# A graph layer on one core: raw input rows gathered in the head, columns copied in two groups of five, single tiles fetched row by row on SyncE

## The chip, the cores and the metric

The kernel runs on one core of one Trainium2 chip. The metric is device time in microseconds of one execution, taken as the median of several runs. A separate execution was profiled; its trace supplies all rows below.

## The reference

12,500 nodes carry 64 features; 412,500 edges, sorted by receiver, carry 32. All is float32.

```python
h = relu(layernorm(x))
msg_in   = concat(h[src], h[dst], edge)            # 64 + 64 + 32
messages = silu(msg_in @ W1 + b1) @ W2 + b2
logits   = silu(msg_in @ Wa1 + ba1) @ Wa2 + ba2
att      = softmax(logits, axis=0)                 # over all edges
agg      = segment_sum(messages * att, dst)
out      = x + silu(concat(h, agg) @ Wu1 + bu1) @ Wu2 + bu2
```

## The kernel before

**Head.** L170 to L313 read x in 8 chunks, normalise it, and transpose it into `hT` (node features in columns, two nodes' features above each other in the 128 partitions). `senders` (L259) multiplies `hT` with the sender half of both first layers and writes one 128-wide row per node to `ts_d` in HBM; the loop at L300 does the same for receivers into `tr_d`, adding the bias, and issues its DMAs from ScalarE's queue. L313 also writes `hT` itself to `hT_d` (used only in a fallback pass).

**Main loop.** The edges lie in tiles of 128, eight tiles to a group, 403 groups. For a group `g`:

- `load(g)` (L524) runs two groups ahead (`AHEAD = 2`). GpSimd issues one indirect DMA for each tile (L533): 128 rows of `ts_d`, chosen by `src`, into the tile `gs`. There are 7 such buffers. SyncE loads the edge features and receiver numbers once per four groups (L544, L547) and two windows of `tr_d` per group (L554) at an address from a register. VectorE builds a one-hot matrix of receivers (L558), and TensorE multiplies it with the window (L562) into `pe` in PSUM.
- `begin(g)` (L570): VectorE adds `pe` and `gs` (L573), ScalarE takes the tanh (L576).
- `end(g)` (L578): VectorE forms the messages and the logits (L586 to L597) in four passes of 512 columns. silu is made of tanh, a sum and a product, on weights that are halved.
- `sum_up` (L714) handles the group five steps older: eight weighted one-hots on VectorE (L640), eight matmuls (L646), a copy of the sum out of PSUM on ScalarE (`out_of`, L652), a projection (L657), and an addition into the running sums in SBUF (`put`, L660).

**Chosen groups.** In every third group (127 of them) the eighth tile isn't gathered. SyncE loads its 128 sender numbers (`numbers`, L474), VectorE turns them into column numbers of `hT` (`places`, L481, six operations), and ScalarE reads these into registers and copies 128 columns of `hT`, one instruction each (`columns`, L504), in six bursts over three steps. One matmul with `stack` (L568) then makes the eighth tile's rows, after VectorE has masked the wrong half (L567). `begin` needs an extra copy for that tile (L575).

**Tail.** After the last group the node update runs over 13 tiles of up to 8 x 128 nodes (L825 to L866): exp of the running maxima (`factor`, ScalarE), a product (`first`, VectorE, two instructions), a sum on GpSimd, tanh and a product (`silu`), matmuls of 128 rows with block-diagonal weights (`second`), and a sum with x (`rest`), then the output DMAs.

**What orders the work.** Each engine and each queue takes its instructions in program order, and nearly all are pinned to the order of the text. A buffer's reuse, a tile's landing and each of the rotating DMA semaphores are waited for at the issuing instruction. So a DMA on SyncE that waits for a buffer holds back everything that SyncE issues behind it.

Of the kernel before, what the change touches and what calls it, by code (L numbers as in the profile page):

```python
# [44 lines left out]
F32 = mybir.dt.float32  # L45
I32 = mybir.dt.int32
# [7 lines left out]
P = 128  # L54
# [14 lines left out]
B = 4  # L69
NQ = 4  # L70
# [3 lines left out]
EVERY = 3  # L74
PHASE = 1
SLOTS = (((0, 24), (24, 24)), ((48, 24), (72, 12)), ((84, 24), (108, 20)))
# [7 lines left out]
PARTS = [("pair", 4 * C), ("we", C), ("bias", C), ("wu2h", 2 * D), ("wa2", U), ("bu2", D), ("w_bu", U),  # L84
         ("w2b", U), ("wu1a", U), ("wu2", D), ("ba2", 1), ("w_bup", 2 * U), ("bu1", 1)]
HALVED = 4
# [4 lines left out]
def gnn_kernel(ctx: ExitStack, tc: tile.TileContext, n_edges, x, src, src_row, dst, dst_row, first, edge,  # L91
# [14 lines left out]
    hT_d = dram.tile([2 * D, NB // 2, P], F32, name="hT_d")  # L106
# [19 lines left out]
    w_bu = part["w_bu"][:D + 1]  # L126
# [25 lines left out]
    nc.vector.memset(zero, 0.0)  # L152

# [8 lines left out]
    gather = ctx.enter_context(tc.tile_pool(name="gather", bufs=7))  # L162


    with tc.tile_pool(name="node1", bufs=1) as node1, \
            tc.tile_pool(name="node", bufs=2) as node, \
            tc.tile_pool(name="node_ps", bufs=2, space=PSUM) as node_ps:
        x_v = x.rearrange("(p b) d -> p b d", b=NB)

# [10 lines left out]
        nc.sync.dma_start(src_full, src)  # L180
# [11 lines left out]
        def windows():  # L192
# [6 lines left out]
            pin(nc.vector.tensor_tensor(dloc[:, T - K:], dloc[:, T - K:], real, ALU.mult))  # L199
            for h in range(2):  # L200
                pin(nc.vector.tensor_scalar(bj[:, :, h], base_full, iota_p, float(SHIFT * h),
                                            op0=ALU.add, op1=ALU.add))
# [13 lines left out]
        def subtract(i):  # L216

            n = chunks[i][1]
            total = node.tile([P, CB], F32, name="total")[:, :n]
            pin(nc.vector.tensor_reduce(total, xcs[i], AX.X, ALU.add))  # L220
            xm = xms[i] = node.tile([P, CB, D], F32, name="xm", bufs=3)[:, :n, :]
            pin(nc.vector.scalar_tensor_tensor(xm, total[:, :, None].to_broadcast([P, n, D]), -1.0 / D,
                                               xcs[i], op0=ALU.mult, op1=ALU.add))
# [34 lines left out]

        def senders(i, first, last):  # L259
# [6 lines left out]
            for b in range(first, last, 4):  # L266
                m = min(4, last - b)
                pn = node_ps.tile([P, 4, C], F32, name="pn", bufs=4)
                for k in range(0, m, 2):
                    pin(nc.tensor.matmul(pn[:, k:k + 2, :], hT[:, (c + b + k) // 2, :],  # L270
                                         w_pair[:, 0], start=True, stop=True))
                pin(nc.scalar.copy(ts[:, b:b + m, :], pn[:, :m, :]))
            if last == nn:
                pin(nc.sync.dma_start(
                    ts_d.rearrange("(p b) f -> p b f", b=NB)[:, c:c + nn, :], tss.pop(i)))

# [5 lines left out]
        for i in range(nch + 1):  # L282
            if i < nch:
                totals(i)
# [12 lines left out]
            if i < nch:  # L297
                normal(i)
        windows()
        for c, nn in chunks:  # L300
            tr = node.tile([P, CB, C], F32, name="tr")[:, :nn, :]
            for b in range(0, nn, 4):
                n = min(4, nn - b)
                pn = node_ps.tile([P, 4, C], F32, name="pn", bufs=4)
                for i in range(0, n, 2):
                    pin(nc.tensor.matmul(pn[:, i:i + 2, :], hT[:, (c + b + i) // 2, :],
                                         w_pair[:, 1], start=True, stop=True))
                pin(nc.vector.tensor_tensor(tr[:, b:b + n, :], pn[:, :n, :],
                                            bias[:, None, :].to_broadcast([P, n, C]), ALU.add))
            pin(nc.scalar.dma_start(  # L310
                tr_d[:NP, :].rearrange("(p b) f -> p b f", b=NB)[:, c:c + nn, :], tr))
        pin(nc.scalar.dma_start(tr_d[NP:, :], zero[:WR, :]))
        pin(nc.scalar.dma_start(hT_d, hT))  # L313
# [6 lines left out]


def node_bias(tc, b, v, work, ps):

    nc = tc.nc
    NB, w_bu = v["NB"], v["w_bu"]
    n = min(4, NB - b)
    hb = work.tile([D + 1, 4, P], F32, name="hb")
    nc.vector.memset(hb[D:, :, :], 1.0)
    for r in range(2):
        nc.sync.dma_start(hb[:D, r:n:2, :], v["hT_d"][r * D:(r + 1) * D, b // 2:(b + n) // 2, :])  # L330
    pb = ps.tile([P, 4, P], F32, name="mt")
    nc.tensor.matmul(pb[:U, :n, :], w_bu, hb[:, :n, :], start=True, stop=True)
    return pb[:U, :n, :]


def tile_bias(tc, c, first, v, work, ps, bus):
# [12 lines left out]
    to = bus[c].rearrange("u (h k p b) -> u k h p b", h=2, k=2, b=m // 2)  # L349
    for b in range(i, i + n):  # L350
        r, k = b % 2, b // (m // 2)
        if b >= i + 2 and m // 2 > 1:
# [3 lines left out]
        at = b - k * (m // 2)  # L356
        pin(nc.vector.tensor_scalar(  # L357
            to[:, k, :, :, at:at + 2 * q - 1:2],
# [12 lines left out]
def halves(ap, c, n, k, NB):  # L371

    return ap.rearrange("(h p b) d -> p h b d", h=2, b=NB)[:, :, c + k * n // 2:c + (k + 1) * n // 2, :]


def tile_rest(tc, c, step, v, work, rest):
# [3 lines left out]
    if step == 0:  # L380
        xt = rest[c] = work.tile([P, 4 * P], F32, name="xt", bufs=1)[:, :n * D]
        for k in range(2):
            nc.sync.dma_start(
                xt[k * P // 2:(k + 1) * P // 2].rearrange("p (h b d) -> p h b d", h=2, d=D),
                halves(v["x"], c, n, k, v["NB"]))
# [8 lines left out]
def one_pass(tc, n_edges, v):  # L394
# [9 lines left out]
    ACTS, WINS, AHEAD = 8, 3, 2  # L404

    starts = list(range(0, NG - 11, B)) + [NG - 11, NG - 9] + list(range(NG - 7, NG))
    NS = len(starts)
# [4 lines left out]
    with ExitStack() as ctx:  # L412
# [6 lines left out]
        bases = keep.tile([33, NG + 1], I32, name="bases")  # L419
        base_lo, base_hi = bases[0:1], bases[32:33]  # L420
        nc.vector.memset(base_lo, 0)
        nc.vector.memset(base_hi, 0)
        nc.vector.tensor_scalar(base_lo[:, :NG], base_sb[:, :NG], float(NH), float(W),
                                op0=ALU.min, op1=ALU.add)
        nc.vector.tensor_scalar(base_hi[:, :NG], base_sb[:, :NG], float(W - NH), 0.0,
                                op0=ALU.add, op1=ALU.max)
        nmax = keep.tile([P, NS + 1], F32, name="nmax")
        nc.vector.memset(nmax[:, 0:1], BIG)
        scale = keep.tile([P, NS], F32, name="scale")
        total = keep.tile([P, 1], F32, name="total")  # L430
        nc.vector.memset(total, 0.0)
        start = keep.tile([P, 2], F32, name="start")
        nc.vector.memset(start[:, 0:1], 0.0)
        nc.vector.memset(start[:, 1:2], BIG)
        ones = keep.tile([P, P], F32, name="ones")
        nc.vector.memset(ones, 1.0)
# [4 lines left out]
        stack = keep.tile([2 * D, C], F32, name="stack")  # L441
        nc.vector.tensor_tensor(stack, v["w_pair"][:, 0, :C], v["w_pair"][:, 0, C:], ALU.add)
        half = keep.tile([P, 1], F32, name="half")
        nc.vector.memset(half[:D], 0.0)
        nc.vector.memset(half[D:], 1.0)
        w2u = keep.tile([S1, 2, U], F32, name="w2u")
        acts = [keep.tile([EP, K, S1], F32, name=f"acts{i}") for i in range(ACTS)]
        for a in acts:
            nc.vector.memset(a[:, :, U:S1], 1.0)
        wins = [keep.tile([P, 2, 2, C], F32, name=f"wins{i}") for i in range(WINS)]  # L450
        for w in wins:
            nc.vector.memset(w, 0.0)
            for r in range(2):
                rows = slice(WR + r * DE, WR + (r + 1) * DE)
                nc.vector.tensor_copy(w[rows, :, r, :], we[rows, None, :].to_broadcast([DE, 2, C]))
        with tc.tile_pool(name="work2", bufs=2) as work2, \
# [3 lines left out]
            pes, gss, lgs, ps_, psums, sps, pps, ees, mts, nums, cols = ({} for _ in range(11))  # L460


            w2t_ps = one_ps.tile([P, 4, P], F32, name="mt")[:U, 0, :S1]
            nc.tensor.transpose(w2t_ps, w2b, ident[:S1, :S1])
            w2t = small.tile([U, S1], F32, name="w2t", bufs=1)
            nc.vector.tensor_copy(w2t, w2t_ps)
            w2u_ps = one_ps.tile([P, 4, P], F32, name="mt")[:S1, 0, :U]
            nc.tensor.matmul(w2u_ps, w2t, wu1a, start=True, stop=True)
            for h in range(2):
                nc.vector.tensor_copy(w2u[:, h, :], w2u_ps)  # L470

            chosen = {g for g in range(8, NG - 12) if g % EVERY == PHASE}

            def numbers(g):  # L474
                if g in chosen:
                    e = (g * K + K - 1) * EP
                    n = nums[g] = small.tile([P, EP], I32, name="num", bufs=2)
                    nc.sync.dma_start(n, bass.AP(tensor=v["src_row"].tensor,
                                                 offset=v["src_row"][:, e:].offset, ap=[[0, P], [1, EP]]))

            def places(g):  # L481
                if g not in chosen:
                    return
                n = nums[g]
                near = small.tile([1, EP], F32, name="near", bufs=1)
                to = small.tile([1, EP], I32, name="to", bufs=2)
# [654 lines left out]
```

## Time and profile before

| | us |
|---|---|
| median of 3 runs | 3992.78 (3986.42 to 3993.82) |
| the profiled execution's own time | 3986.92 |
| its span in the trace | 3985.1 |
| PE / weight loads busy | 2332.9 / 1888.3 |
| VectorE (DVE) busy | 3264.8 |
| ScalarE (ACT) busy | 2173.0 |
| GpSimd (POOL) busy | 2950.2 |

Busy leaves out instructions that only read registers, branch, wait or issue a DMA from SP or ACT; the indirect DMAs on POOL are counted as busy. "Idle before" in a group's row is the time in which its engine did nothing before an instruction of that group, with what ended it; "issue" means that it waited for nothing that the trace shows. SPq is SyncE's queue, PEld the weight loads. L numbers are lines of the kernel before.

### The profile page before, as it was taken

How to read it: one execution, taken by the hardware profiler on the slowest of the kernel's cores; microseconds unless marked ns; L12 is line 12 of the kernel's file. 1: busy time of each engine (PE TensorE's matmuls, PEld its weight loads, DVE VectorE, ACT ScalarE, POOL GpSimd, SP SyncE). 2: the span in 40 equal slices, each digit the busy share in tenths (PEclk: the TensorE clock that was granted, in tenths of full speed). 3: DMA queues.
4: the chain of work that ended last, by engine and by line, in shares of the span. 5: the costliest groups of instructions: out<-in, count | busy, mean ns of one | idle time of the engine just before them, and what ended most of it. 6: DMA issues, size and time to landing. Idle time of an engine off the chain costs nothing. (4 is left out here: it accounts for less than half of the span.)

```text
span 3985.1 us, 80416 instructions
## 1 busy us (share of the span) xinstructions
PE 2332.9 (59%) x11238; PEld 1888.3 (47%) x11238; DVE 3264.8 (82%) x9553; ACT 2173.0 (55%) x17477; POOL 2950.2 (74%) x3122
## 2 busy tenths in 40 slices
PE   6556566666666555555555555555655555555566
PEld 5444444454444444444444444444544444444455
DVE  6888888888888787888878888887878887878787
ACT  3655555555555555555555555555555555555512
POOL 3777777777777777777777777777777777777774
PEclk8766666666666666666666666666666665666666
DMA  8333343333333333333333333333333333333333
GB/s 287 101 99 99 95 110 92 103 99 102 102 92 95 93 85 93 87 92 88 89 94 84 95 93 86 94 84 94 88 91 94 84 95 87 91 95 84 104 105 85
DMA packets 219778, 391.64 MB, mean 98 GB/s; under 512 B 72209, under 2 KB 146898, under 8 KB 206050
## 3 DMA queue, kind: packets, MB, share of 16 engines
q0 software_dynamic: 99104, 203.16, 19.1%
q1 hardware_dynamic: 118754, 173.60, 16.7%
q10 hardware_dynamic: 1376, 9.67, 0.6%
q14 instruction: 452, 3.70, 0.3%
q8 instruction: 92, 1.51, 0.2%
HBM read 360.42 MB, written 25.72 MB: 97 GB/s over the span
## 5 line engine op out<-in xcount | busy, mean ns | idle before, releaser
L533 POOL DMA_INDIRECT gs<-ts_d,src_sb x3097 | 2933.0, 947 | 992.6 <-issue 854.1
L562 PE MATMUL pe<-wins,eo 128*128 128x256 f32 x3224 | 1465.1, 630 | 925.7 <-DVE eo L558 679.6
L504 ACT COPY cols<-hT 128x1 f32 x16256 | 1605.0, 187 | 717.7 <-issue 714.8
L562 PEld LDWEIGHTS pe<-wins,eo 128*128 128x128 f32 x3224 | 970.9, 318 | 1222.7 <-DVE eo L558 769.0
L576 ACT ACTIVATE pe<-gs 128x1024 f32<-128x1024 f32 x403 | 413.7, 1026 | 928.6 <-DVE gs L573 496.8
L573 DVE TENSOR_TENSOR gs<-pe,gs 128x1024 f32<-128x1024 f32 (+1 forms) x403 | 475.4, 1180 | 393.6 <-DMA gs<-ts_d,src_sb 369.2
L640 DVE TENSOR_SCALAR wt<-iota_w,dloc,p 128x40 f32<-128x40 f32 x3224 | 726.1, 321 | 1.8
L646 PE MATMUL sp<-wt,acts 128*65 128x40 f32 x6448 | 628.8, 268 | 6.3 <-DVE wt L640 3.9
L646 PEld LDWEIGHTS sp<-wt,acts 128*65 128x65 f32 x6448 | 589.9, 183 | 16.2 <-DVE wt L640 9.7
L657 PEld LDWEIGHTS mt<-ss,w2u 65*128 65x128 f32 x806 | 203.0, 279 | 336.2 <-issue 173.9
L657 PE MATMUL mt<-ss,w2u 65*128 65x40 f32 x806 | 181.6, 319 | 242.3 <-DVE gm L623 202.0
L616 PE MATMUL mt<-ident,mx 128*128 128x128 f32 x107 | 47.4, 443 | 445.8 <-DVE sums L675 427.2
L594 DVE TENSOR_TENSOR pe<-pe,w_all 128x512 f32<-128x512 f32 x403 | 281.8, 699 | 13.4
L558 DVE TENSOR_SCALAR eo<-dbs,bj 64x256 f32<-64x256 int32 x806 | 277.9, 375 | 18.2 <-DMA dbs<-in_dst_row_dram 9.0
L592 DVE SCALAR_TENSOR_TENSOR pe<-pe,gs 128x512 f32<-128x512 f32 x403 | 280.3, 696 | 10.5
L586 DVE SCALAR_TENSOR_TENSOR acts<-pe,gs 128x512 f32<-128x512 f32 x403 | 277.2, 688 | 12.4 <-ACT pe L576 3.2
L597 DVE TENSOR_REDUCE lg<-pe 128x8 f32<-128x512 f32 x403 | 277.0, 687 | 10.5
L616 PEld LDWEIGHTS mt<-ident,mx 128*128 128x128 f32 x107 | 19.5, 182 | 456.9 <-issue 455.0
L678 DVE COPY stand<-nmax 64x40 f32 x806 | 161.0, 200 | 3.2
L671 DVE SCALAR_TENSOR_TENSOR sums<-sums,scale,mt 64x40 f32 x214 | 54.2, 253 | 89.2 <-PE mt L657 85.0
L675 DVE TENSOR_TENSOR sums<-sums,mt 64x40 f32 x592 | 111.5, 188 | 4.7 <-PE mt L657 0.6
L357 DVE TENSOR_SCALAR bu<-mt,w_all 64x256 f32<-64x256 f32 (+1 forms) x50 | 23.9, 477 | 88.7 <-PE mt L348 88.3
(124 smaller groups left out, 1062.7 us busy)
## 6 DMA issues: line engine op xcount, KB each, us to landing
eo<-in_edge_dram SPq DMA_DIRECT2D x100, 512.0 KB
dbs<-in_dst_row_dram SPq DMA_DIRECT2D x200, 256.0 KB
gs<-ts_d,src_sb POOLq DMA_INDIRECT x3097
wins<-tr_d SPq DMA_DIRECT2D x806, 32.0 KB
num<-in_src_row_dram SPq DMA_DIRECT2D x127, 64.0 KB
ts_d<-ts SPq DMA_DIRECT2D x5, 896.0 KB
tr_d<-tr ACTq DMA_DIRECT2D x5, 896.0 KB
hT_d<-hT ACTq DMA_DIRECT2D x1, 3136.0 KB
```

The costliest lines, as they stand in the source:

```text
L504: pin(nc.scalar.copy(to[:, first + i:first + i + 1], hT[:, bass.ds(regs[i], 1)]))
L533: nc.gpsimd.indirect_dma_start(out=full[:rows, j, :], out_offset=None, in_=ts_d[:, :], in_offset=bass.IndirectOffsetOnAxis(ap=src_full[:ro ...
L558: pin(nc.vector.tensor_scalar(eo[:WR, e], db[:, e], bj[g // NQ % 2 * WR:(g // NQ % 2 + 1) * WR, g, h:h + 1], None, op0=ALU.is_equal))
L562: pin(nc.tensor.matmul(pe[:, 2 * q:2 * q + 2, :], eo[:, q * EP:(q + 1) * EP], win[:, q // 2, :, :], start=True, stop=q < H - 1 or g not in ...
L573: pin(nc.vector.tensor_tensor(gss[g][:, :n, :], pes[g][:, :n, :], gss[g][:, :n, :], ALU.add))
L576: pin(nc.scalar.activation(pes[g], gss[g], AF.Tanh))
L586: pin(nc.vector.scalar_tensor_tensor(acts[g % ACTS][:, :, 0:U], th[:, :, U:C], 1.0, gs[:, :, U:C], op0=ALU.add, op1=ALU.mult))
L592: pin(nc.vector.scalar_tensor_tensor(att, th[:, :, 0:U], 1.0, gs[:, :, 0:U], op0=ALU.add, op1=ALU.mult))
L594: pin(nc.vector.tensor_tensor(att, att, wa2[:EP, None, :].to_broadcast([EP, K, U]), ALU.mult))
L640: pin(nc.vector.tensor_scalar(wt[:, j, :], iota_w[:EP, j // H, :], dloc[:, g * K + j:g * K + j + 1], p[:, k + j:k + j + 1], op0=ALU.is_equ ...
L646: pin(nc.tensor.matmul(sp, acts[g % ACTS][:, j, :], wt[:, j, :], start=j == 0, stop=j == K - 1))
L657: pin(nc.tensor.matmul(pp, w2u.rearrange("s h u -> s (h u)"), sps.pop(g), start=True, stop=True))
```

## The change

Five things are changed at once.

1. **Raw rows in the head.** The first four groups (`RAW = 4`) no longer use `ts_d`. In the head GpSimd gathers 32 tiles of 64-wide rows of x itself, into two of the gather buffers; ScalarE and VectorE normalise them, TensorE transposes them, and in `load(g)` for `g < 4` four more matmuls with `w_pair` make the senders' part. `gather` has 6 buffers in place of 7, `acts` 6 in place of 8; `begin` writes to a tile `sm` of its own, so that a gather buffer is free after `begin`, not after `end`.
2. **Columns in two of five groups**: 153 groups in place of 127 (`g % 5` 0 or 3, from 10 on), in ten equal half steps. The column numbers are made once, before the loop, for all groups (`column_lists`: two rounds of load, six VectorE operations, two stores to `list_d`); per chosen group SyncE then fetches one row of numbers (`listed`) and one broadcast row of parities (`parity`).
3. **Rows on SyncE**: in one group of eleven (33 by the formula in the code, 22 to 374) the eighth tile is fetched by 128 DMAs of one 512-byte row each, addressed by registers, 12 per step, spread over the eleven steps before.
4. **The head and out_of**: constants are set up early; the sender and receiver matmuls are split into halves of 64 rows; `tr_d` is written from SyncE; `hT_d` is gone; the copy out of PSUM in `out_of` moves from ScalarE to VectorE.
5. **Tail**: all 13 exps first and in place, one product per tile, ScalarE's `Silu` in place of tanh and a product, matmuls of 64 rows, one output layout for both halves.

```diff
-EVERY = 3
-PHASE = 1
-SLOTS = (((0, 24), (24, 24)), ((48, 24), (72, 12)), ((84, 24), (108, 20)))
+EVERY = 5
+LEADS = {0: 9, 3: 10}
+SLOTS = ((0, 28), (28, 24), (52, 28), (80, 24), (104, 24))
+FIRST = 10
+ROWS = 12
+SPAN = -(-EP // ROWS)
+RAW = 4
...
+        for g in range(RAW):
+            for j in range(K):
+                nc.gpsimd.indirect_dma_start(
+                    out=raws[g // 2][:, g % 2, j, :], out_offset=None, in_=x[:, :],
+                    in_offset=bass.IndirectOffsetOnAxis(ap=src_full[:, g * K + j:g * K + j + 1], axis=0))
...
+        def rows_of(pn, r, c, m):
+            for k in range(m // 2):
+                for h in range(2):
+                    rows = slice(h * D, (h + 1) * D)
+                    pin(nc.tensor.matmul(pn[:, h, k, :], hT[rows, c // 2 + k, :],
+                                         w_pair[rows, r, h * C:(h + 1) * C], start=True, stop=True))
...
+        def raw_squares(a):
+            flat = raws[a].rearrange("p r k d -> p (r k) d")
+            spare = node_ps.tile([P, 4, P], F32, name="pt")[:, 0, :D]
+            for i in range(RD):
+                pin(nc.scalar.activation(spare, flat[:, i, :], AF.Square, bias=raw_sum[a][:, i:i + 1],
+                                         accum_out=raw_sq[a][:, i:i + 1]))
...
-        pin(nc.scalar.dma_start(hT_d, hT))
...
+            def rows(g):
+                r, i = (g + 2) // SPAN + 1, (g + 2) % SPAN
+                of = [c for c in rowed if c // SPAN == r]
...
+                at, n = i * ROWS, min(ROWS, EP - i * ROWS)
...
+                loads, regs = nc.values_load_multi_w_load_instructions(
+                    places[of[0]][0:1, at:at + n], engines=[ENG.SP], min_val=0, max_val=NP - 1,
...
+                for k in range(n):
+                    pin(nc.sync.dma_start(single[of[0]][at + k:at + k + 1, :], ts_d[bass.ds(regs[k], 1), :]))
...
-                for j in range(K - (g in chosen)):
+                for j in range(0 if g < RAW else K - (g in chosen or g in rowed)):
...
+                    if g < RAW:
+                        turned = v["raws"][g // 2][:, g % 2].rearrange("p k d -> p (k d)")
+                        pin(nc.tensor.matmul(pe[:, 2 * q:2 * q + 2, :], turned[:, q * EP:(q + 1) * EP],
+                                             v["w_pair"][:, 0], start=False, stop=True))
...
+                sm = sms[g] = work2.tile([EP, K, C], F32, name="sm", bufs=2)
...
-                pin(nc.scalar.copy(ss, sp))
+                pin(nc.vector.tensor_copy(ss, sp))
...
-                numbers(g + 7)
-                places(g + 6)
+                listed(g + 9)
+                rows(g)
+                asked(g + SPAN + 5)
+                parity(g + 5)
...
-                pin(nc.scalar.activation(th, ut, AF.Tanh, scale=0.5))
-                pin(nc.vector.scalar_tensor_tensor(ut, th, 1.0, ut, op0=ALU.add, op1=ALU.mult))
+                pin(nc.scalar.activation(ut, ut, AF.Silu))
...
-                    pin(nc.tensor.matmul(po[:, i, :, :], uv[:, i], wu2h, start=True, stop=True))
+                    for h in range(2):
+                        rows = slice(h * U, (h + 1) * U)
+                        pin(nc.tensor.matmul(po[:, h, i * D:(i + 1) * D], uv[rows, i],
+                                             wu2h[rows, h, :], start=True, stop=True))
```

More of the change, by code (lines that the diff above doesn't have):

```diff
@@ L265, in senders @@
             ts = tss[i]
[L266 to L272, printed above, removed]
+            for b in range(first, last, 8):
+                m = min(8, last - b)
+                pn = node_ps.tile([P, 2, 4, C], F32, name="pn", bufs=3)
+                rows_of(pn, 0, c + b, m)
+                pin(nc.scalar.copy(ts[:, b:b + m, :].rearrange("p (k h) c -> p h k c", h=2), pn[:, :, :m // 2, :]))
             if last == nn:
@@ L403, in one_pass @@
         v[k] for k in ("wa2", "ba2_c", "w2b", "wu1a", "wu2h", "we", "gather"))
[L404 to L407 removed]
+    AHEAD = 2
+    starts, NS, nmax, total, start, ones, half, bases, acts, wins, stack, w2u = (
+        v[k] for k in ("starts", "NS", "nmax", "total", "start", "ones", "half", "bases", "acts", "wins",
+                       "stack", "w2u"))
     batch = [sum(1 for i in starts if i <= g) - 1 for g in range(NG)]
@@ L459, in one_pass @@
                 tc.tile_pool(name="one_ps", bufs=1, space=PSUM) as one_ps:
[L460 to L468, printed above, removed]
@@ L496, in columns @@
-            def columns(g, first, n):
-                if g not in chosen:
-                    return
-                to, at = cols[g]
-                _, regs = nc.values_load_multi_w_load_instructions(
-                    at[0:1, first:first + n], engines=[ENG.Activation], min_val=0, max_val=NP // 2 - 1,
+            pes, gss, lgs, ps_, psums, sps, pps, ees, mts, lists, odds, cols, sms, single, places = ({} for _ in range(15))
+            chosen = [g for g in range(FIRST, NG - 12) if g % EVERY in LEADS]
@@ new lines, in columns @@
+            def columns(g, first, n):
+                if first == 0:
+                    cols[g] = small.tile([P, EP], F32, name="cols", bufs=2)
+                loads, regs = nc.values_load_multi_w_load_instructions(
+                    lists[g][0:1, first:first + n], engines=[ENG.Activation], min_val=0, max_val=NP // 2 - 1,
+                    skip_runtime_bounds_check_because=WHY)
+                for one in loads:
+                    pin(one)
+                for i in range(n):
+                    pin(nc.scalar.copy(cols[g][:, first + i:first + i + 1], hT[:, bass.ds(regs[i], 1)]))
```

334 lines of the change are left out of this document (194 added, 140 removed).

## The prediction

> **What bounds the kernel now.** First the page: the span and the busy times, then the costliest group, then the waits of POOL and DVE, then the timeline around the first and the last gather.
>
> ```profile
> span 3985.1 us, 80416 instructions
> PE 2332.9 (59%) x11238; PEld 1888.3 (47%) x11238; DVE 3264.8 (82%) x9553; ACT 2173.0 (55%) x17477; POOL 2950.2 (74%) x3122
> L533 POOL DMA_INDIRECT gs<-ts_d,src_sb x3097 | 2933.0, 947 | 992.6 <-issue 854.1
> ```
> ```profile
> POOL gs L533 <- issue: 854.1, 2802, 0.3
> ...
> DVE gs L573 <- DMA gs<-ts_d,src_sb: 369.2, 175, 6.5
> ...
> POOL gs L533 <- DMA ts_d<-ts: 47.4, 1, 47.4
> POOL gs L533 <- DMA gs<-ts_d,src_sb: 46.9, 149, 1.8
> ```
> ```profile
> 49.82 1.10 POOL L533 DMA_INDIRECT gs<-ts_d,src_sb  x1 [47.43 <-DMA ts_d<-ts]
> ...
> 3927.03 0.94 POOL L533 DMA_INDIRECT gs<-ts_d,src_sb  x1 [0.30 <-issue]
> ```
>
> DVE has the highest share, yet it waits 369.2 us for gathers, while POOL hardly waits for anybody: its idle time is 0.3 us of issue behind nearly each gather, one wait for `ts_d`, and 46.9 us in all for earlier gathers to land. From first to last gather pass 3877.2 us, 1.2523 us for each of 3096 steps. So the stream of gathers on POOL is the time: 49.8 us ahead of it, 3877.2 in it, and 58.1 from the last gather to the end. A group costs 3097/403 x 1.2523 = 9.62 us.
>
> **The change, part by part.**
>
> *Fewer gathers.* 3224 tiles less 32 (raw), 153 (columns) and 33 (rows) leave 3006 in the stream, 91 fewer than before. The groups from 10 on have 2958; at 1.2523 a step of these groups costs 9.43 us on average, 8.77 where a tile is left out. Whether POOL stays the bound depends on the other engines' steps.
>
> *DVE.* It loses `places`, gains `out_of`, and 26 more masks and copies.
>
> ```profile
> L567 DVE SCALAR_TENSOR_TENSOR cols<-num,half,cols 128x128 f32<-128x128 int32 x127 | 43.6, 343 | 2.0
> L490 DVE TENSOR_SCALAR near<-near 1x128 f32<-1x128 f32 x127 | 37.4, 294 | 4.3
> L492 DVE SCALAR_TENSOR_TENSOR to<-to,near 1x128 int32<-1x128 int32 x127 | 36.3, 286 | 4.3
> L575 DVE COPY gs<-pe 128x128 f32<-128x128 f32 x127 | 35.5, 280 | 0.0
> L491 DVE TENSOR_SCALAR near<-near 1x128 f32<-1x128 f32 x127 | 32.7, 257 | 4.3
> ...
> L487 DVE TENSOR_SCALAR to<-num 1x128 int32<-1x128 int32 x127 | 32.4, 255 | 2.0
> L489 DVE TENSOR_SCALAR near<-to 1x128 f32<-1x128 int32 x127 | 31.4, 247 | 4.3
> ...
> L493 DVE TENSOR_SCALAR num<-num 128x128 int32<-128x128 int32 x127 | 27.4, 216 | 0.0
> ...
> L466 DVE COPY w2t<-mt 64x65 f32<-64x65 f32 x1 | 0.2, 208 | 0.0
> ```
> ```profile
> L573 DVE TENSOR_TENSOR gs<-pe,gs 128x1024 f32<-128x1024 f32 x276 | 337.2, 1222 | 345.2 <-DMA gs<-ts_d,src_sb 325.5 <-issue 14.2 <-PE pe L562 4.4
> ...
> L573 DVE TENSOR_TENSOR gs<-pe,gs 128x896 f32<-128x896 f32 x127 | 138.2, 1088 | 48.4 <-DMA gs<-ts_d,src_sb 43.6
> ```
>
> `places` is L487 and L489 to L493: 197.6 us go. `out_of` adds 403 x 0.208 = 84. The new groups add 26 x (0.343 + 0.280 - 0.134) + 33 x (0.280 - 0.134) = 18. DVE ends near 3170 busy, 7.9 us a step. Nothing of this is on the path, since 9.43 covers it.
>
> *ACT.* It loses `out_of` and gains 26 x 128 column copies.
>
> ```profile
> L504 ACT COPY cols<-hT 128x1 f32 x16256 | 1605.0, 187 | 717.7 <-issue 714.8 <-DVE pe L592 2.9
> ...
> L576 ACT ACTIVATE pe<-gs 128x1024 f32<-128x1024 f32 x403 | 413.7, 1026 | 928.6 <-DVE gs L573 496.8 <-DVE gs L575 238.9 <-DMA gs<-ts_d,src_sb 187.9
> ```
>
> A chosen group costs (1605.0 + 717.7)/127 = 18.29 us with its register reads; 153 cost 2798. With tanh 413.7 and about 75 us of small exps that is 3287, or 8.2 us a step. The 928.6 us that ACT waited ahead of tanh shrink by about half, and 1.2 us a step remain. Queued behind a late burst is the next tanh, and DVE's messages wait for that; between `begin` and the messages DVE has the one-hots of two later steps to make (L558, L640), which hide a tanh that is late by a little.
>
> *SP.* Each of 363 steps (9 to 371) gets 11.6 row DMAs and a read of 12 registers.
>
> ```profile
> L554 SPq FUSED_REGOPS  x806: 37/37/51, 78.2 to 3889.7; - x162
> L554 SPq MOVE wins<-tr_d x806: 29/29/123, 78.3 to 3889.8; - x162
> L554 SPq DMA_DIRECT2D wins<-tr_d x806: 316/317/1517, 78.4 to 3889.8; - x162
> ```
> ```profile
> L547 SPq DMA_DIRECT2D dbs<-in_dst_row_dram x202: 332/412/1539, 74.0 to 3836.9; - x101
> ```
> ```profile
> 2003.74 0.85 SPq L554 DMA_DIRECT2D wins<-tr_d  x2
> 2003.78 1.21 ACT L504 COPY cols<-hT 128x1 f32 x12 [0.73 <-issue]
> ```
>
> A DMA at a register's address takes 37 + 29 + 317 ns, 0.38 us, at least; two of them took 0.85 us from the first's start to the second's end, so one follows another after 0.53. The trace has no one-row DMA; the two-window DMA is the nearest row, and I take 0.52. Twelve registers cost ACT 0.73 us. SP's step: windows 1.04, rows 6.05, registers 0.78, `listed` and `parity` 0.36, a quarter of the three loads and four registers 0.45: **8.7 us**, with 7.1 and 10.0 as ends: 0.38 a row without any gap, and 0.63 where a row is as slow to issue as `dbs` (412 ns for 317). I stay by the windows because they too take their address from a register. The step fits in 9.43 by 0.7, and the upper end does not. Behind a stuck row stand the next windows, for which PE waits, and behind PE `begin`. `listed` adds a wait for ACT's register reads three chosen groups back, `parity` one for DVE's mask two back; the twelve rows of the step and the next windows queue behind them. SP runs ahead of PE by up to three windows, so a stall of a few us now and then is covered; a step above 9.43 is not.
>
> The Trainium skill ("DMA: Bandwidth & Descriptors", Rules for kernel authors) speaks against this part: many small transfers should be coalesced, and below 64 KB one pays mostly overhead; its Anatomy of one DMA fits about 2.0 us fixed for a DMA (from GpSimd). One after another, 11.6 of them would make a step of some 26 us and a kernel far above 9000. The two windows' 0.85 us show that SP doesn't wait for one landing before the next issue, so the sum doesn't use it.
>
> *Head.* 32 raw gathers take 32 x 1.25 = 40 us and fit in POOL's 47.4 us wait. But `load(8)` and `load(9)` reuse the raw rows' buffers, and `load(10)` waits for `begin(4)`: the stream may start early, but compute now sets when it goes on.
>
> ```profile
> 71.27 0.71 ACTq L313 DMA_DIRECT2D hT_d<-hT  x1
> ...
> 90.79 8.16 PE L562 MATMUL pe<-wins,eo 128*128 128x256 f32 x24 [22.68 <-DMA wins<-tr_d]
> ...
> 94.58 1.23 DVE L573 TENSOR_TENSOR gs<-pe,gs 128x1024 f32<-128x1024 f32 x1 [4.44 <-PE pe L562]
> ...
> 106.14 1.21 DVE L573 TENSOR_TENSOR gs<-pe,gs 128x1024 f32<-128x1024 f32 x1
> ...
> 111.25 1.21 DVE L573 TENSOR_TENSOR gs<-pe,gs 128x1024 f32<-128x1024 f32 x1
> ```
>
> Without stops `load(10)` would begin at 49.8 + 48 x 1.2523 = 110. Compute: PE starts near 94 (before 90.8; two rounds of lists ahead of the loads cost up to 10, the store of `hT` at 71.27, which ran beside them, is gone). 8 matmul records cost 8.16/3 = 2.7 us, twice that for a raw group: `begin(0)` near 99.5, then some 6.3 a step in place of 5.1, with a transpose of the second raw buffer between: `begin(4)` near 125, and `load(10)` at **126**, between 110 and 140. DVE's two reductions for the raw rows are 1024 columns each, about 1.2 us like L573's. ACT's raw statistics are 96 instructions of 64 columns, 18 us at 0.187 and 29 at 0.3; ACT idled 49.6 us there (the table's row below). `tr_d`'s stores now queue on SP ahead of the lists, but the first loads wait for the same buffers. The 64-row senders and constants may move `ts_d` by some us; the 16 us between 110 and 126 cover that.
>
> *Tail.*
>
> ```profile
> 3943.42 0.69 ACT L830 ACTIVATE pe<-stand,nmax 128x512 f32<-128x512 f32 x1
> ...
> 3946.31 0.87 DVE L838 SCALAR_TENSOR_TENSOR gs<-sums,inv,pe 128x256 f32<-128x256 f32 x2
> ...
> 3948.70 0.60 ACT L848 ACTIVATE pe<-gs 128x512 f32<-128x512 f32 x1 [1.71 <-POOL gs L843]
> 3949.34 0.69 DVE L849 SCALAR_TENSOR_TENSOR gs<-pe,gs 128x512 f32<-128x512 f32 x1 [1.37 <-ACT pe L848]
> ...
> 3961.04 2.14 PE L856 MATMUL pe<-w_all,hT 128*128 128x128 f32 x8
> ...
> 3976.84 0.28 DVE L862 TENSOR_TENSOR gs<-pe,gs 128x128 f32<-128x128 f32 x1
> ```
> ```profile
> L576 ACT ACT_TABLE_LOAD x1 | 1.3, 1283 | 49.6 <-DMA gs<-ts_d,src_sb 49.6
> ```
>
> A tile costs DVE 0.87 + 0.69 + 0.69 = 2.25 now and 1.5 after. But all exps come first (12.3 x 0.69 = 8.5 from 3943.4) and a table load (1.28): the first silu starts near 3953.2, 4.5 later. PE's 2.14 a tile then sets the pace, as two half matmuls replace one: 13 tiles end near 3953.2 + 0.6 + 13 x 2.14 + 0.7 = 3982, 5 late; by DVE's 1.5 they would end 3 early, and at twice PE's price 30 late. I take **+2**. The Trainium skill ("TensorE: Matmul & The Clock Gate", Part 3: Packing small matmuls) has weight loads overlap running matmuls only where the row groups differ, as the halves' do; by it the tail would come out near the early end, 5 us less in the sum. No run here shows it.
>
> *Sum.* Last gather at 126 + 2957 x 1.2523 = 3829; 58.1 + 2 behind it: span 3889, the execution 1.8 more (3986.9 against 3985.1), 3891. The median shown lies 5.9 above the profiled execution: **3897**. All other edits (the constants' places, `tile_bias`' layout, `xt`'s) keep the counts and are free while POOL is the bound.
>
> **Rivals.**
>
> *SP becomes the pace-setter (slower).* Time = 3897 + 363 x (S - 9.43) for SP's step S; it passes the old 3993 at S = 9.69, 0.61 us a row. At the upper end of 0.63 S is 10.0 and the time 4104. For it: 0.09 us more a row, one more wait on a semaphore for instance, is enough, and nothing hides it, because it comes back in 363 steps. Against: 0.53 measured between two DMAs of the same kind, with 64 pieces each where a row has one.
>
> *ACT and DVE pace each other.* If no register read hides behind a tanh, two bursts (26 copies at 1605.0/16256 = 0.099 and a read of 0.73 x 26/12 each) with tanh and exps cost 5.1 + 3.2 + 1.2 = 9.5 a step, just over POOL's: 126 + 398 x 9.5 + 60, and 8 for the rest, about 3975. Against: the 18.29 above holds the reads as they were, with one of each two beside a tanh.
>
> *The raw rows don't do what they are there to do.* POOL's 40 us of early gathers count only as far as compute follows. Before, `load(10)` came behind 80 gathers, at 49.8 + 80 x 1.2523 = 150. If lists, statistics and the doubled matmuls put `begin(4)` there, the stream goes on as late as before and only the 3017 - 2958 = 59 gathers fewer from group 10 on remain: 3897 + 24 = 3921.
>
> **How the numbers follow.** Forecast 0.57, raw rows bring nothing 0.10, ACT and DVE 0.14, SP 0.19. The forecast's own range is 3865 to 3927 (head -16 to +14, tail -5 to +28, a few us of pitch). The range reaches to the ACT case and leaves out SP's: 3862 to 3980. A measurement tells 0.2% (8 us) from no change. Faster: 0.57 + 0.10 + 0.11 of the third = 0.78; within 0.2%: 0.03; slower: 0.19.
>
> **What would show it.** POOL still idle by 0.3 us of issue alone in the loop, near 3038 gathers, one stop between 90 and 126; DVE near 3170 busy and waiting for gathers; SP's row DMAs 0.5 apart, and no wait of PE for windows. Wrong if PE or DVE wait for `wins` or `single`, if POOL waits for `begin`'s buffers past the first 20 groups, or if tanh waits for ACT's own bursts.

## The result, and the profile after

The changed kernel takes 3934.62 us (median of 4 runs, 3933.72 to 3936.31) against 3993.18 (3986.42 to 3993.82) for the kernel before on the same chip: a ratio of 0.9856, 95% interval 0.984 to 0.9871. It is 58.6 us faster; 96 were forecast. The profiled execution took 3934.74 us, its span 3933.0.

The page and its costliest groups, as shown of before (in the group lines: busy us, mean ns, idle ahead and what ended it):

```profile
span 3933.0 us, 99304 instructions
PE 2330.5 (59%) x11632; PEld 1910.5 (49%) x11632; DVE 3151.7 (80%) x9249; ACT 2440.6 (62%) x20500; POOL 2907.9 (74%) x3063
L622 POOL DMA_INDIRECT gs<-ts_d,src_sb x3006 | 2851.9, 949 | 967.7 <-issue 824.5
L568 ACT COPY cols<-hT 128x1 f32 x19584 | 1919.0, 187 | 886.8 <-issue 776.3
L675 ACT ACTIVATE pe<-sm 128x1024 f32<-128x1024 f32 x403 | 410.7, 1019 | 493.3 <-DVE ss L751 236.8
```

The busy times are close to the predicted ones: DVE 3151.7 against 3170, ScalarE's column copies with the idle time ahead of them 2805.8 against 2798. POOL's timeline at four places: the first gather of the stream, the first of `load(8)`, the first of `load(10)`, the last of all.

```profile
52.89 0.95 POOL L622 DMA_INDIRECT gs<-ts_d,src_sb  x1 [2.54 <-issue]
...
107.96 0.95 POOL L622 DMA_INDIRECT gs<-ts_d,src_sb  x1 [15.36 <-issue]
...
128.75 0.95 POOL L622 DMA_INDIRECT gs<-ts_d,src_sb  x1 [0.96 <-DVE sm L670]
...
3869.01 0.95 POOL L622 DMA_INDIRECT gs<-ts_d,src_sb  x1 [0.30 <-issue]
```

Against the predicted sum (126, 3703, 60.1): `load(10)` is 2.8 us late; the stream from there takes 3869.01 - 128.75 = 3740.3, 37 too many; behind the last gather pass 64.0, 3.9 too many. Together 44, the whole of 3933.0 - 3889.

Where do the 37 lie? Two windows of 900 us, before and then after. Behind the window's length stand the busy times of PE, PEld, DVE, ACT and POOL, each with its instructions in brackets (POOL's are the gathers), then the granted clock of TensorE, the DMA share and the GB/s:

```profile
400.00:1300.00 900.00, 546.13 (x2575) 435.29 (x2576) 769.11 (x2253) 515.35 (x4278) 681.15 (x719) 0.64 0.38 98
1300.00:2200.00 900.00, 514.30 (x2528) 417.21 (x2527) 731.56 (x2168) 513.43 (x4270) 680.83 (x720) 0.64 0.35 91
```
```profile
400.00:1300.00 900.00, 526.77 (x2529) 422.06 (x2530) 721.90 (x2128) 559.68 (x4866) 656.83 (x691) 0.64 0.38 97
1300.00:2200.00 900.00, 544.81 (x2680) 450.10 (x2678) 744.51 (x2217) 601.54 (x5248) 680.97 (x719) 0.65 0.37 94
```

Elsewhere 719 or 720 gathers fit into 900 us, but only 691 here: 28 x 1.25 = 35 us lost. In that stretch, called the stretch from here on, POOL waits for the buffers that `begin` frees (us in total, how often, the longest; L751 is the instruction behind `begin` on DVE):

```profile
POOL gs L622 <- DVE sm L674: 21.7, 13, 3.9
POOL gs L622 <- DVE ss L751: 13.0, 7, 3.1
```

So the compute step sets the pace there. What DVE waited for in the same 900 us, before and after:

```profile
DVE bu L357 <- PE mt L348: 69.8, 20, 4.6
DVE sums L671 <- PE mt L657: 19.7, 15, 1.6
DVE gs L573 <- DMA gs<-ts_d,src_sb: 11.6, 15, 4.7
```
```profile
DVE bu L449 <- PE mt L441: 84.1, 20, 6.0
DVE sums L770 <- PE mt L756: 42.9, 21, 4.2
DVE acts L685 <- ACT pe L675: 11.0, 13, 1.1
DVE ss L751 <- PE sp L745: 4.9, 8, 0.7
```

`bu` is `tile_bias`, the node bias that groups 16 to 119 evaluate on the side. After, busy time and these waits make 721.90 + 142.9 = 864.8 us for 92 groups: 9.4 a group, just what POOL needs (9.43); with smaller waits and gaps the 900 us come to 9.8. Before, busy time and the waits for PE made 769.11 + 89.5 for 95 groups, 9.0 against POOL's 9.62. One such step in the timeline:

```profile
830.22 3.75 PE L651 MATMUL pe<-wins,eo 128*128 128x256 f32 x8 [1.61 <-DVE eo L647]
...
833.77 1.06 PE L441 MATMUL mt<-hT,w_all 128*128 128x256 f32 x2
...
834.87 0.98 DVE L449 TENSOR_SCALAR bu<-mt,w_all 64x256 f32<-64x256 f32 x2 [4.42 <-PE mt L441]
```

The bias' matmul stands on PE behind eight edge matmuls, and DVE, next in whose order is the evaluation, waits 4.42 us for it.

### The profile page after: what moved, and what is told of

Same layout as the page of the kernel before. It is cut to its first block, busy times and chain, and to the rows that moved or that the text cites. A ratio compares the mean times of both kernels' runs of the same rounds, so it can differ in the third digit from the quotient of the medians.

```text
span 3933.0 us, 99304 instructions
## 1 busy us (share of the span) xinstructions
PE 2330.5 (59%) x11632; PEld 1910.5 (49%) x11632; DVE 3151.7 (80%) x9249; ACT 2440.6 (62%) x20500; POOL 2907.9 (74%) x3063
## 4 chain that ended last, share of the span: by engine, by line
issue 20%; POOL 20%; DVE 20%; DMA 13%; ACT 10%; PE 10%; SPq 4%; ACTq 2%; DVEq 1%; POOLq 0%
POOL gs L622 20%; DMA gs<-ts_d,src_sb 9%; ACT cols L568 7%; PE pe L651 6%; DVE wt L739 5%; DVE sm L670 2%; SPq L592 2%; ACT pe L675 2%; DVE pe L691 2%; DMA dbs<-in_dst_row_dram 2%; DVE acts L685 2%; DVE pe L693 2%; DVE eo L647 2%; ACTq L562 2%; DVE lg L696 1%
## 5 line engine op out<-in xcount | busy, mean ns | idle before, releaser
L622 POOL DMA_INDIRECT gs<-ts_d,src_sb x3006 | 2851.9, 949 | 967.7 <-issue 824.5
L568 ACT COPY cols<-hT 128x1 f32 x19584 | 1919.0, 187 | 886.8 <-issue 776.3
L651 PEld LDWEIGHTS pe<-wins,eo 128*128 128x128 f32 x3224 | 991.9, 323 | 1253.4 <-issue 709.5
L675 ACT ACTIVATE pe<-sm 128x1024 f32<-128x1024 f32 x403 | 410.7, 1019 | 493.3 <-DVE ss L751 236.8
L670 DVE TENSOR_TENSOR sm<-pe,gs 128x1024 f32<-128x1024 f32 (+1 forms) x399 | 462.3, 1159 | 202.4 <-DMA gs<-ts_d,src_sb 182.4
L745 PE MATMUL sp<-wt,acts 128*65 128x40 f32 x6448 | 613.8, 266 | 5.2 <-DVE wt L739 3.7
L745 PEld LDWEIGHTS sp<-wt,acts 128*65 128x65 f32 x6448 | 577.9, 181 | 11.6 <-DVE wt L739 7.6
L685 DVE SCALAR_TENSOR_TENSOR acts<-pe,sm 128x512 f32<-128x512 f32 x403 | 278.0, 690 | 59.9 <-ACT pe L675 51.2
L691 DVE SCALAR_TENSOR_TENSOR pe<-pe,sm 128x512 f32<-128x512 f32 x403 | 281.6, 699 | 13.1
L647 DVE TENSOR_SCALAR eo<-dbs,bj 64x256 f32<-64x256 int32 x806 | 265.4, 366 | 15.8 <-DMA dbs<-in_dst_row_dram 7.9
```

The costliest lines, as they stand in the source:

```text
L568: pin(nc.scalar.copy(cols[g][:, first + i:first + i + 1], hT[:, bass.ds(regs[i], 1)]))
L622: nc.gpsimd.indirect_dma_start(out=full[:rows, j, :], out_offset=None, in_=ts_d[:, :], in_offset=bass.IndirectOffsetOnAxis(ap=src_full[:ro ...
L647: pin(nc.vector.tensor_scalar(eo[:WR, e], db[:, e], bj[g // NQ % 2 * WR:(g // NQ % 2 + 1) * WR, g, h:h + 1], None, op0=ALU.is_equal))
L651: pin(nc.tensor.matmul(pe[:, 2 * q:2 * q + 2, :], eo[:, q * EP:(q + 1) * EP], win[:, q // 2, :, :], start=True, stop=g >= RAW and (q < H - ...
L670: pin(nc.vector.tensor_tensor(sm[:, :n, :], pes[g][:, :n, :], gs[:, :n, :], ALU.add))
L675: pin(nc.scalar.activation(pes[g], sm, AF.Tanh))
```

## The experiments

Theory: that wait lifts the compute step over the stream's 9.43, and the stretch costs 37 us. Rivals: ScalarE's bursts pace it; SyncE's rows land its inputs late. Ratios are to the kernel before on the same chip (3985 to 3998 us there); the changed kernel's is 0.9856.

**1. The bias' matmul earlier** (`tile_bias` cut in two).

```diff
+                if biased:
+                    pb = tile_bias_product(tc, (g // 8 - 2) * NC, g % 8 == 1, v, work2, one_ps, bus)
                 if g + AHEAD < NG:
                     load(g + AHEAD)
...
-                    tile_bias(tc, (g // 8 - 2) * NC, g % 8 == 1, v, work2, one_ps, bus)
+                    tile_bias(tc, (g // 8 - 2) * NC, g % 8 == 1, v, pb, bus)
```

> One edit to the changed kernel: the matmul of the node bias (L441) is issued ahead of the eight edge matmuls of load(g + 2), its DVE evaluation (L449) stays where it was. Theory: in groups 16 to 119 DVE waits 4.2 us for that matmul 24 times (100.9 us in all), this lifts the compute step over the 9.43 us that POOL needs for a group, and the gather pitch of 1.3046 us between 400 and 1300 us is the price, some 37 us. Then the wait on mt falls below 1 us each, the pitch in that window returns to 1.253, and the time is 3898 to 3908 us. Rival A, ScalarE's bursts of column copies pace that stage by themselves: the wait moves to another line, the pitch stays above 1.29, 3930 to 3938. Rival B, SyncE's rows land the inputs late there: the same 3930 to 3938.

3892.01 us, ratio 0.9764 (0.9749 to 0.9779). The window and the wait:

```profile
400.00:1300.00 900.00, 542.13 (x2692) 446.22 (x2692) 768.08 (x2252) 596.25 (x5199) 680.59 (x719) 0.65 0.40 102
```
```profile
DVE bu L461 <- PE mt L441: 5.5, 11, 0.7
```

691 gathers have become 719, and the ratio fell by 0.0092, 37 us. Moving this one matmul brings the whole loss back, with ScalarE's bursts and SyncE's rows as they were: neither rival makes the loss by itself.

**2. The bias spread** over 24 groups in place of 8, its matmul where it was.

```diff
-                if g >= 16 and g // 8 - 2 < NT and g % 8 in (1, 5):
+                if g >= 16 and (g - 16) // 24 < NT and (g - 16) % 24 in (3, 15):
```

> One edit to the changed kernel: each of the 13 node-bias chunks is spread over 24 groups in place of 8 (evaluations 12 groups apart, groups 16 to 327), the matmul stays behind load's. Theory: the waits of DVE on mt remain, 4 us each, but only one in 12 groups, which six gather buffers cover: the mean compute step falls below 9.43, the gather pitch is 1.253 throughout and the time 3898 to 3910 us. Rival A (ScalarE's bursts) and rival B (SyncE's rows): nothing moves, 3930 to 3938, pitch between 400 and 1300 us still above 1.29.

3891.11 us, 0.9764 (0.9749 to 0.9779): the same gain, with each wait for the bias' matmul left as it was (8 in the stretch, 3.9 us on average). The edit also spreads the rest of the side work (`tile_rest`, `tile_bias_out`) over the 24 groups. It is the mean step that counts.

**3. No rows.**

```diff
-            rowed = [r * SPAN + (r * SPAN % EVERY in LEADS) for r in range(2, (NG - 13) // SPAN)]
+            rowed = []
```

> One edit to the changed kernel: no group fetches its last tile by rows, the 33 are gathered by POOL again. Theory (rows cost nothing but SyncE's idle time; POOL is the bound outside groups 37 to 120): 33 gathers by 1.2525 are 41 us, less the 7 to 8 rowed groups that lie where the compute step is the bound (9 us or so): 3963 to 3972 us. Rival B (SyncE's rows are what slows the stretch of 400 to 1300 us): that stretch gets its 37 us back, so that the loss is only 5 us: 3934 to 3945, with the gather pitch there at 1.253.

3958.36 us, 0.9933 (0.9918 to 0.9948): 31 us slower than the changed kernel by the ratio, within the 28 to 37 foreseen, and the stretch keeps its stalls (702 gathers). The rows are worth 31 us, and the loss isn't theirs.

**4. The head in another order.**

```diff
+        for a in range(1, RAW // 2):
+            raw_means(a)
+            raw_squares(a)
         for c, nn in chunks:
+            if c == chunks[min(2, nch - 1)][0]:
+                raw_scales(0)
+                raw_normal(0)
```

> One edit to the changed kernel, in the head: sums and squares of both raw pairs come first (ScalarE has them done before the receivers' table), the scales, reluing and turning of both inside the loop over the receivers' chunks, so that DVE no longer waits 5.29 us on raw_dev at 57.26 us and again 5.11 at 89.00, and the tiles of the edges (whose place in the memory is that of the head's eps) are free when the receivers' table is stored. Theory: begin(0) moves from 103.8 to about 93 us, POOL's stop at load(8) shrinks from 15.4 us to 5, and as the stream sets the end, the time falls by 8 to 11 us: 3923 to 3927. Rival: the index rows land late for another cause (the gathers of POOL beside them): begin(0) at 99 to 100, 3930; or the stretch of 400 to 1300 us swallows what is won, 3934.

3922.85 us, 0.9845 (0.9832 to 0.9859): the intervals overlap. In the trace `begin(0)` came at 100.4 (near the first rival's 99 to 100) and `load(10)` at 125.25, 3.5 us earlier; the stretch stayed as it was. Most of the hoped-for gain was missed: TensorE now stopped for the raw rows' turning inside the loop, and the index rows landed only at 92.1.

**5. No raw rows** (`RAW = 0`, their code left out).

> The changed kernel without its raw rows: the first four groups gather rows of the senders' table like all others, so the stream has 3038 gathers in place of 3006. By the changed kernel's trace gather 48 started at 128.75 us after a stop of 15 us; without raw rows six buffers hold groups 0 to 5 and begin(0) comes before the 48 gathers are out, so that gather 48 starts at 50 + 48 x 1.2525 = 110 and no stop is left. Of the 40 us that 32 gathers cost, 19 come back: 21 us slower than the changed kernel, a ratio of 0.9905 to 0.992 to the kernel before. Rival (raw rows bring nothing, since their own work holds up the head): a ratio of 0.985 to 0.987.

3935.75 us, 0.9843 (0.9828 to 0.9858): not 21 us slower but level. The theory of this run was wrong in what it left out. Gather 48 was reached without a stop, as foreseen (at 113.10 us), but in the stretch fewer gathers were lost (710 in the window, against 691). The last stall of both traces, changed kernel first:

```profile
1209.14 0.94 POOL L622 DMA_INDIRECT gs<-ts_d,src_sb  x1 [2.94 <-DVE sm L674]
```
```profile
1210.70 0.95 POOL L615 DMA_INDIRECT gs<-ts_d,src_sb  x1 [2.94 <-DVE sm L667]
```

Counted through the traces these are the same tile (882 gathers of the stream lie ahead of it, and 914 of one with 32 more). Compute leaves the stretch within 1.6 us of the same time either way, so a lead that POOL had won ahead of it is gone.

**6. The copy of the sums back on ScalarE.**

```diff
-                pin(nc.vector.tensor_copy(ss, sp))
+                pin(nc.scalar.copy(ss, sp))
```

> One edit to the changed kernel: the copy of a group's sums out of PSUM goes back from DVE to ScalarE. Theory: between 400 and 1300 us the chain of DVE with its wait for PE is the bound; 0.19 us of DVE for each of about 85 groups is worth up to 16 us there and nothing elsewhere: the ratio falls from 0.9856 to 0.982 to 0.985. Rival: the copy then sits behind ScalarE's bursts and DVE waits for it through PE, so that the stretch gets longer: 0.987 to 0.995.

3897.56 us, 0.9752 (0.9737 to 0.9767): 41 us, over twice the upper end expected. The window, and DVE's longest waits in it:

```profile
400.00:1300.00 900.00, 583.98 (x2688) 468.53 (x2686) 746.08 (x2134) 603.38 (x5250) 681.31 (x718) 0.61 0.39 101
```
```profile
DVE bu L449 <- PE mt L441: 74.8, 18, 4.9
DVE sums L770 <- PE mt L756: 34.8, 24, 3.0
```

718 gathers again, though each wait for the bias is as long as it was. The expectation counted the copy's 0.19 us alone; busy time and waits fell from 9.4 to some 8.9 us a group (746.08 + 109.6 and 8.2 of two further waits for PE, for 97 groups), since the waits for PE and ACT fell too. That is under 9.43, and no stall is left. So the wait for the matmul and the copy on DVE cost 37 us together; with either of them gone, the other costs nothing there. The rest lies behind the last gather (59.4 in place of 64.0).

**7. Both: the early matmul and a mended head** (on 1 and 4: the turning behind the loop, the index rows in memory of their own and loaded early).

```diff
+            for g in range(AHEAD):
+                load(g)
             column_lists()
-            for g in range(AHEAD):
-                load(g)
```

> The early matmul of the node bias (first experiment) with the head of the fourth, mended at two places: the raw pair is turned behind the receivers' loop, so that TensorE does not wait there, and the index rows have a place of their own in the memory, are loaded before the receivers' table, and column_lists comes behind the first two loads. Theory: the two gains lie in different stages and add up; begin(0) comes at 88 to 94 us in place of 103.8, the stop before load(8) falls from 15 us to under 6, and the ratio falls from the first experiment's 0.9764 to 0.973 to 0.975. Rival: the stop moves to load(10), whose buffer begin(4) frees, and nothing is won over the first experiment: 0.976 to 0.978.

3890.07 us, 0.9733 (0.972 to 0.9746). `begin(0)` and `load(8)`'s first gather:

```profile
95.19 1.23 DVE L687 COPY sm<-pe 128x1024 f32<-128x1024 f32 x1 [2.45 <-PE pe L675]
```
```profile
99.30 0.94 POOL L641 DMA_INDIRECT gs<-ts_d,src_sb  x1 [6.33 <-issue]
```

Both miss their marks by a little (88 to 94, under 6), the ratio does not. The stop is 6.3 us in place of 15.4, `load(10)` starts at 120.03 against 130.88 in experiment 1: 11 us, and the ratio's 0.0031 is 12.

**8. Sixteen rows a group** on 7 (`ROWS = 16`).

> The kernel of e7_head_bias with 16 rows per group in place of 12, so that a tile takes 8 groups and 46 groups have their last tile fetched by rows in place of 33. Theory: SyncE has room (a row costs 0.40 to 0.42 us, not the 0.52 of my sum, so that its step is 7.5 us and becomes 9.1, under the 9.43 of POOL's group): 13 gathers fewer, 16 us less, a ratio 0.004 below e7's. Rival, SyncE becomes the pace-setter: with the waits on its own DMAs its step passes 9.4 us, the windows land late and the kernel is 10 to 60 us slower than e7.

4349.29 us, 1.0879 (1.0864 to 1.0894). The rival came true, far beyond its price. What PE waits for, and the rows of one step (here, then in the changed kernel):

```profile
PE pe L670 <- DMA wins<-tr_d: 1139.2, 238, 12.8
```
```profile
1610.98 6.47 SPq L611 DMA_DIRECT2D single<-ts_d  x16
```
```profile
1612.05 4.82 SPq L592 DMA_DIRECT2D single<-ts_d  x12
```

A row takes 0.40 us in both. With 16 of them a group takes 10.5 us (76 groups between 1400 and 2200 us): the rows' 6.5, the register read's 1.2, windows, lists, and waits of SyncE for its own DMAs (32.5 us in these 76 groups, 0.4 each), which the sum of 9.1 had left out; the other 1.0 above that sum was not taken apart. 1.1 us too many in 368 groups is 405 of the 459 us by which it is slower than 7.

**9. Experiment 7 with the copy on ScalarE.**

> The kernel of e7_head_bias with the copy of the sums back on ScalarE (e6). Theory: the stretch of 400 to 1300 us has no stall left to win (pitch 1.253 in e7), so the only gain is at the end, where e6 took 59.5 us from the last gather to the end and the kernels with the copy on DVE 63 to 65: 4 to 5 us, a ratio of 0.9715 to 0.973 beside e7's 0.9733. Rival: the two gains of the stretch add up like those of different stages, some 30 us more: 0.964 to 0.967.

3886.91 us, 0.9731 (0.9718 to 0.9744): no difference from 7 that the times can tell. In the trace the end behind the last gather takes 59.25 us in place of 64.33, which agrees. It and 7 are the shortest versions and beat both kernels.

**10. The early matmul without raw rows** (1 with 5).

> The early matmul of the node bias (e1) without raw rows (e5). Theory: the raw rows do bring their 19 to 21 us (32 gathers of 1.25 less the stop of 15 to 16 us before load(8) and the later start), but in the changed kernel the stretch in which the compute step is the bound swallows them; without that stretch's wait they show: a ratio 0.0045 to 0.0055 above e1's 0.9764, 0.981 to 0.982. Rival: the raw rows are worth nothing in any kernel, since what they save is what they hold up: 0.9755 to 0.9775.

3922.24 us, 0.9821 (0.9806 to 0.9836): 0.0057 above experiment 1, 23 us, where 18 to 22 were expected. The raw rows are worth what they should be, once nothing behind them takes it back.

**11. Thirteen rows** on 9 (`ROWS = 13`).

> The kernel of e9_best_act with 13 rows per group in place of 12: ten groups for a tile, 37 tiles by rows in place of 33. In e8 SyncE set the pace at 10.6 us a group with 16 rows; a row and its register are 0.46 us of it (0.40 and 0.06), so 12.8 rows per group give 9.1 us and 11.6 (the changed kernel) 8.6, both under the 9.43 of the stream. Theory: 4 gathers fewer, 5 us less than e9, a ratio lower by 0.001. Rival: the steps that issue the edges' blocks too already pass the six buffers' room, and the kernel is 10 us or more slower than e9.

4177.31 us, 1.046 (1.0446 to 1.0474), 290 us slower than 9: the rival came true, but not for the cause that it names. SyncE's register read, here and in 8 (ns: lowest, median, highest):

```profile
L605 SPq TENSOR_LOAD <-asked x370: 974/2857/3057, 126.3 to 3898.2; - x185
```
```profile
L605 SPq TENSOR_LOAD <-asked x368: 973/1166/1856, 117.9 to 4023.7; - x184
```

Thirteen words took 2.86 us where sixteen took 1.17; 1.7 us more is enough to lift most steps over 9.43, as the sum of 9.1 left 0.3 (between 1400 and 2200 us a group takes 10.0). Of a tile's ten reads the first, fifth and ninth (from word 0, 52 and 104) took 1.0 to 1.25, the others 2.5 to 3.0.

**12. Columns in one group of five.**

```diff
-LEADS = {0: 9, 3: 10}
+LEADS = {0: 9}
```

> The changed kernel with columns in one of five groups in place of two: 77 groups in place of 153, so 76 gathers more, 95 us of the stream at 1.2525. Theory: the stream then needs 9.68 us a group, the compute step between 400 and 1300 us is hardly above it, and the 37 us of stalls go: 95 - 37 = 58 us slower than the changed kernel, a ratio of 0.999 to 1.002. Rival: ScalarE's bursts in that stretch, not DVE's chain, make the stalls, and the tanh waits go with them: below 0.997. Rival: the stalls have nothing to do with the stream's step and stay: 1.007 to 1.011.

3991.31 us, 0.9993 (0.9984 to 1.0003), as the theory has it: 76 gathers cost 95 us, the stretch gives back its stalls (719 gathers in its window), and 55 remain. DVE's wait for the bias stayed (84.0 us in the window, against 84.1) though ScalarE's bursts were halved, but its wait for the projections (`sums`) fell from 42.9 to 16.3. This run changes the stream's step and the bursts at once, so it doesn't tell which of the two freed the stretch, nor whether the bursts had a part in the loss.

## Why the prediction was right, and where it was 37 us out

- **The bound, right.** The time is the stream's outside the stretch: from gather 883 at 1209.14 us to the last, the 3006th, at 3869.01 a step takes 1.2529 us, 1.2523 predicted; runs 3, 10 and 12 moved with their gathers, less what stalls gave back.
- **DVE: the step that failed.** "DVE ends near 3170 busy, 7.9 us a step. Nothing of this is on the path, since 9.43 covers it." The busy time was right. But 7.9 is a mean over the whole span and holds no wait; between 400 and 1300 us DVE's step with its waits for PE is 9.4 and more. Before's own window showed it: 858.6 of 900 us busy or waiting for PE, only 11.6 waiting for gathers. The change took 0.2 us from what POOL leaves a group, took `places` off DVE, and put a copy on it that PE's projection waits for; waits for PE and ACT rose from 89.5 to 142.9 us. Runs 1, 2 and 6 each remove the loss alone. Whether a seventh gather buffer, which the change gave up, would have covered the stretch was not tried. No term of the sum and no rival held this loss: the time came out beyond the forecast's own 3865 to 3927, in the part that had been added for ACT and DVE, another mechanism. One of the prediction's own signs of being wrong shows it: POOL waited for `begin`'s buffers far past the first 20 groups.
- **The head, right by 2.8 us, not in its parts.** PE started at 97.9, not 94. DVE's rows of the head and two of other engines:

```profile
57.26 0.25 DVE L358 RECIPROCAL raw_dev<-raw_dev 128x16 f32<-128x16 f32 x1 [5.29 <-ACT raw_dev L355]
...
88.66 0.31 ACT L355 ACTIVATE raw_dev<-raw_sq,eps 128x16 f32<-128x16 f32 x1
88.99 0.53 SPq L633 DMA_DIRECT2D eo<-in_edge_dram  x1
...
97.34 1.13 DVE L647 TENSOR_SCALAR eo<-dbs,bj 64x256 f32<-64x256 int32 x4 [7.88 <-DMA dbs<-in_dst_row_dram]
...
103.78 1.23 DVE L668 COPY sm<-pe 128x1024 f32<-128x1024 f32 x1 [5.31 <-PE pe L656]
```

  ACT's statistics were not hidden under its idle time: they stood between DVE and the receivers' table (5.29 us), and the edges' first block was issued the moment ACT had read `eps` for the last time. That the block waited for `eps`' memory is argued from the order and fits run 7, which did several things at once. Against that, `begin(4)` came soon enough that the stop was 15 us, as foreseen.
- **The raw rows.** The rival that they bring nothing (3921) came true in effect, by another mechanism: their 23 us are won in the head and lost in the stretch (5 and 10).
- **ACT, right.** It set no pace by itself (1) and held up DVE directly for only 11.0 us in the stretch. Through PE it may have done more: there PE waited 46.5 us for a tanh ahead of its edge matmuls, a wait that before's window doesn't have. In run 1 it is 7.5 with ScalarE's work unchanged, so ScalarE's load alone doesn't make it. The rival of ACT and DVE pacing each other came nearest in kind: a compute step of 9.5 or more (9.8 measured), but with DVE and PE in it, and in 104 groups, not 398.
- **SP, right in the verdict, the size too high.** One row follows another after 0.41 us, not 0.52 (16 take 6.47 and 12 take 4.82), and a register read takes 0.94, not 0.78; POOL's pace outside the stretch shows that the step stays under 9.43. PE did wait for windows, where none was foreseen (the prediction names such a wait as a sign of being wrong):

```profile
PE pe L651 <- DMA wins<-tr_d: 58.9, 17, 5.4
```

  Run 3, without rows, is 31 us slower and keeps the stalls, so this cost nothing that the time tells. The price beyond the limit was rightly feared: 8 and 11. The Trainium skill ("DMA: Bandwidth & Descriptors", Rules for kernel authors) warns of many small transfers; here 4224 of 0.5 KB gained 31 us, since another queue had the time, and with 16 a group in place of 12 the kernel was 459 us slower.
- **The tail, +2 predicted.** From the exps on it takes 42.7 us, 1.0 more than before. PE's tile:

```profile
3921.42 2.13 PE L955 MATMUL pe<-w_all,hT 64*128 64x64 f32 x16
```

  Sixteen halves are recorded as long as eight whole matmuls were (2.14), but the tiles follow each other faster: from 3909.68 to 3921.42 pass six, 1.96 us each, and before from 3954.48 to 3967.61 also six, 2.19 each, with a short wait for DVE ahead of a tile. Over 13 tiles this is 3 us. The two were not run at one clock (windows as above; the third number from the end is the granted clock), before and after:

```profile
3950.00:3980.00 30.00, 25.69 (x98) 23.54 (x98) 23.90 (x48) 13.27 (x22) 13.18 (x11) 0.73 0.45 106
```
```profile
3900.00:3925.00 25.00, 23.85 (x196) 23.59 (x196) 16.43 (x23) 7.11 (x13) 11.89 (x10) 0.50 0.34 118
```

  The Trainium skill ("TensorE: Matmul & The Clock Gate", Part 3: Packing small matmuls) has weight loads overlap running matmuls where the row groups differ, which the prediction reckoned as 5 us; whether that has a part in the faster pace stays open. The other 4.9 us lie ahead of the exps: the last groups' chain on DVE has the copy in it, and with the copy on ScalarE (6, 9) the whole end takes 59.4 and 59.3.

## What to carry to other kernels

Make the comparison of the bound with the others per stage, on busy time plus waits for other engines, not on mean busy time: an engine that waits for a partner is as full as a busy one. Buffers between two engines make a threshold: below it a longer step costs nothing, above it a gain won earlier is taken back. So undo causes one by one: each may be worth the whole, as in 1, 2 and 6, and their gains don't add up (9). Place a side job's matmul ahead of the long run whose result its reader doesn't need.

## What the hardware showed unexpectedly

A read of 13 words into SyncE's registers took 2.86 us where 12 took 0.94 and 16 took 1.17; within one tile it was short only where the first word's number was divisible by four. That this is the cause wasn't tried by itself. Row DMAs at register addresses follow each other after 0.41 us, in groups of 12 as of 16.
